# Windowed attention in three 128-row query-key passes, a quadrant output projection, single-window value steps and a new step order

## The chip, the cores and the metric

The kernel runs on one core of a Trainium2 chip. The metric is the device time of one execution in microseconds, the median of the runs shown. Engines are named as in the profile: PE (TensorE matmul), PEld (TensorE weight load), DVE (VectorE), ACT (ScalarE), POOL (GpSimd), SP (SyncE).

## The reference

Four residual layers act on x of shape (8, 56, 56, 192), each on a group-normalized copy of it. The change is in layer 1, a windowed attention with 7 x 7 windows, 6 heads of 32 channels and a shift of 3 rows and 3 columns. Its core, cut to what matters:

```python
x = (x - mu) * rsqrt(var + EPS) * gamma + beta            # over 192 channels
sx = roll(x, shift=(-3, -3))                               # rows, columns
win = windows of sx                                        # (windows, 49 tokens, 192)
q, k, v = split(win @ w_qkv + b_qkv)                       # 6 heads x 32 channels each
attn = (q * 32 ** -0.5) @ k.T + rel_bias + mask            # (49, 49) for each head and window
out = softmax(attn) @ v
out = out @ w_proj + b_proj                                # 192 to 192
x = x + roll(out, shift=(3, 3))
```

Everything is float32.

## The kernel before

The four layers run one after another as stages. Layer 1 takes about the stretch from 1985 to 3035 us of the profiled execution. An image lies in SBUF as 128 partitions: 64 channels of the upper image half (s = 0) on partitions 0 to 63 and the same channels of the lower half (s = 1) on 64 to 127, with three channel blocks j. A **group** g, one of four per image, is a strip of seven rows in each half: eight windows for each s. A window row of 49 tokens has two windows, z = 0 and 1, side by side in each of four slots k. So 8 images make 32 groups.

The steps of layer 1 have letters, and a string `plan` (line 1504) gives the order in which they are written down for one group:

- Q (`project(which, m)` in `layer1_scores`): queries or keys, 96 output rows at a time, so four steps per group. Each is 3 x 2 matmuls of 392 columns into two PSUM tiles of the tag `mm`, one for each s, and a copy of each into `qk`. Lines 877 (matmul), 883, 885 and 887 (copies).
- V (`values(k0)`): values of two slots, tokens on partitions. Lines 895 (matmul), 902 and 904 (copies).
- E (`scores(s)`): loads a bias-and-mask tile `bm` with a DMA on SP (line 910), 48 small matmuls into the single PSUM tile `S` (913), then on DVE the add of `bm` (919) and the row maximum (921), and on POOL the subtraction of the maximum (922).
- X (`exponents`): the exponential on ACT (926). Y (`shares`): sum and reciprocal on DVE (931, 932), scaling by the reciprocal on POOL (933).
- T (`turn`): transposes of the shares into PSUM tiles of the tag `et` (954), three steps for each s, the middle one evicted by DVE (961), the others by ACT (959).
- P (`mix`): shares times values into two `et` tiles (968), evicted into `oa` by ACT (979) and DVE (981).
- R (`project(j)` in `layer1_mix`): the output projection of one channel block (987), whose result DVE adds to `x` (995).
- G (`statistics`): group statistics of the strip on DVE (998).
- N: one step of `layer1_norm`, which prepares the next image: 33 steps per image. For strips 0 and 1 and then again for strips 2 and 3: four steps of window copies on POOL (eight instructions, 797), two steps of squares on ACT (804), both twice, and one step with the statistics matmuls (835, 839) and their reduction (850). Then three steps with clamp, square root and reciprocal (810, 812, 814), and four that multiply the image by it (819, 824). The normalization of image b+1 is spread over the groups 0, 1 and 2 of image b; image 0's lies ahead of the loop, and the last image's groups have none.

X, Y, T, P, R and G of a pass through the plan belong to group g, while Q, V and E already prepare group g+1. PE, ACT, DVE and POOL take their instructions strictly in the order in which the steps are written (`manual_schedule`), each engine from its own queue; DMAs have queues of their own. The tag `mm` has three PSUM tiles that rotate among Q, V, R, the statistics and the normalization's broadcasts (`rstd`); the tag `et` has two, which rotate among T and P. A tile is taken again only when the copies out of the tile three (or two) places earlier are done.

`layer1_weights` prepares weights and biases in layer 0's stage, and the host function at the end lays out the weights.

Of the kernel before, what the change touches and what calls it, by code (L numbers as in the profile page):

```python
# [19 lines left out]
HC = 96  # L20
# [9 lines left out]
HEADS, HD, WN = 6, 32, 49  # L30
PW, GW = 64 + WN, 4 * (64 + WN)
# [41 lines left out]
    ("g1", 3), ("be1", 3), ("bq", 2), ("bv", 2), ("bpr", 3),  # L73
# [18 lines left out]
def kernel(ctx: ExitStack, tc: tile.TileContext, a: dict, out: bass.AP):  # L92
# [603 lines left out]
    def layer1_weights(pool, psum):  # L696
# [9 lines left out]
        bv = pool.tile([HC, 2], F32, name="bv", bufs=1)  # L706
        for which, t in ((0, bq), (2, bv)):
            ps = psum.tile([128, 2, 512], F32, name="bias", tag="qv")[:, 0]
            for m in range(2):
                c0 = which * C + HC * m  # L710
                for j in range(3):
                    nc.tensor.matmul(
                        ps[0:HC, m:m + 1], w_qkv[0:64, j, c0:c0 + HC], vec("be1", j, 64), start=(j == 0), stop=(j == 2)
                    )
            o = VOFF["bq" if which == 0 else "bv"]
            nc.vector.tensor_tensor(t, ps[0:HC, 0:2], vecs[0:HC, o:o + 2], ALU.add)
# [3 lines left out]
        for s in range(2):  # L720
            for j in range(3):
                for m in range(2):
                    nc.tensor.matmul(
                        ps[64 * s:64 * s + 64, j:j + 1], w_proj[:, m, 64 * j:64 * j + 64], bv[:, m:m + 1],
                        start=(m == 0), stop=(m == 1),
                    )
# [4 lines left out]
        nc.vector.tensor_scalar(w_qkv[:, :, 0:C], w_qkv[:, :, 0:C], HD ** -0.5, None, ALU.mult)  # L731
# [132 lines left out]
    def layer1_scores(g, xr, pool, psum, S, es, consts):  # L864
# [3 lines left out]
        qk = [pool.tile([HC, 2, 2, TT], F32, name=f"qk{s}", bufs=1) for s in range(2)]  # L868
# [3 lines left out]
        def project(which, m):  # L872
            ps = [psum.tile([128, 512], F32, name="qk_ps", tag="mm", bufs=3)[0:HC, 0:TT] for s in range(2)]
            c0 = which * C + m * HC
            for j in range(3):
                for s in range(2):
                    nc.tensor.matmul(  # L877
                        in_pairs(ps[s]), wg[64 * s:64 * s + 64, j, c0:c0 + HC],
                        in_slots(xr[64 * s:64 * s + 64], (3 * g + j) * GW), start=(j == 0), stop=(j == 2),
                    )  # L880
            for s in range(2):
                if which == 0:
                    nc.scalar.activation(qk[s][:, 0, m], ps[s], AF.Identity, bias=bq[:, m:m + 1])
                elif s == 0:
                    nc.scalar.copy(qk[s][:, 1, m], ps[s])
                else:
                    nc.vector.tensor_copy(qk[s][:, 1, m], ps[s])

        def values(k0):
            ps = [psum.tile([128, 512], F32, name="v_ps", tag="mm", bufs=3)[:, 0:2 * C] for s in range(2)]  # L890
            for k in range(2):
                for j in range(3):
                    for s in range(2):
                        t0 = (3 * g + j) * GW + PW * (k0 + k)
                        nc.tensor.matmul(
                            ps[s][:, C * k:C * k + C], xr[64 * s:64 * s + 64, t0:t0 + 128],
                            wg[64 * s:64 * s + 64, j, 2 * C:3 * C], start=(j == 0), stop=(j == 2),
                        )
            for s in range(2):
                dst = v[s][:, k0:k0 + 2].rearrange("p w c -> p (w c)")  # L900
                if s == 0:
                    nc.scalar.copy(dst, ps[s])
                else:
                    nc.vector.tensor_copy(dst, ps[s])

        mxs = [None, None]
# [21 lines left out]
        def shares(s):  # L928
# [8 lines left out]
            Q=[lambda which=which, m=m: project(which, m) for which in range(2) for m in range(2)],  # L937
            V=[lambda k0=k0: values(k0) for k0 in (0, 2)], E=each(scores),
# [829 lines left out]
```

## Time and profile before

| | us |
|---|---|
| median of 3 runs | 5648.63 (5647.63 to 5649.4) |
| profiled execution, its own time | 5648.44 |
| its span, first to last instruction | 5646.6 |
| layer 1, about | 1985 to 3035 |
| PE busy in the span | 5131.2 (91%) |
| DVE busy | 3030.6 (54%) |
| ACT busy | 2287.3 (41%) |
| POOL busy | 1839.5 (33%) |
| mean granted TensorE clock | 0.961 |

The span is that of the profiled execution, from which all durations come. A matmul in float32 shows as two instructions, so 768 matmuls of a kind are 1536 rows. Busy PE counts overlapping matmuls once, and their ends are modelled, so the price of a step is better read from the start of one step to the start of the next. A row of a timeline gives start, duration, engine, line, operation, out<-in with shapes, the count, and in brackets the idle time of that engine just before and what ended it; neighbouring instructions of one line are merged into one row.

### The profile page before, as it was taken

Reading aid. Unit: us, or ns where it says so; the run is one execution under the profiler, and the core shown is the slowest. Engines: PE = TensorE matmul, PEld = TensorE weight load, DVE = VectorE, ACT = ScalarE, POOL = GpSimd, SP = SyncE. Lnnn points to the kernel's source line nnn. Section 1 sums busy time; section 2 is a strip of 40 time slices with the busy share of each in tenths; the row PEclk is TensorE's granted clock in tenths of the full one; section 3 lists DMA queues with packets and bytes.
Section 4 is the critical chain, followed back from the end, with each engine's and each line's share of the span. In section 5 each row is a group of like instructions: output and inputs, shape, how many; then the busy total and the mean of one; then the engine's idle time right before and its main releaser. Section 6 shows DMA issues by size and latency. Waiting matters only on the chain. (4 is left out here: it accounts for less than half of the span.)

```text
span 5646.6 us, 113339 instructions
## 1 busy us (share of the span) xinstructions
PE 5131.2 (91%) x49446; PEld 3421.6 (61%) x49446; DVE 3030.6 (54%) x4087; ACT 2287.3 (41%) x3100; POOL 1839.5 (33%) x1583
## 2 busy tenths in 40 slices
PE   7899969999999789999997989998888797999999
PEld 6798866666666445555554756775344697444444
DVE  4565534555554456556665868888787103433331
ACT  3344445555555333333331025554667201333333
POOL 5565655555555233334431023333010101101000
PEclk9999979999999889999998999999999898999999
DMA  5988996777777512223225756676677686212211
GB/s 148 235 226 227 223 299 245 272 273 272 273 273 274 151 36 80 74 73 81 75 62 144 266 213 228 231 241 190 185 205 212 247 330 257 78 59 78 80 39 26
DMA packets 556148, 1013.75 MB, mean 180 GB/s; under 512 B 256104, under 2 KB 479684, under 8 KB 528884
## 3 DMA queue, kind: packets, MB, share of 16 engines
q1 hardware_dynamic: 542896, 956.63, 52.8%
q0 software_dynamic: 8512, 40.62, 2.2%
q10 hardware_dynamic: 4244, 9.26, 0.6%
q8 instruction: 389, 6.37, 0.5%
q14 instruction: 107, 0.88, 0.0%
HBM read 676.92 MB, written 345.97 MB: 181 GB/s over the span
## 5 line engine op out<-in xcount | busy, mean ns | idle before, releaser
L460 POOL COPY lc<-lt 128x896 f32<-128x896 f32 (+1 forms) x320 | 590.3, 1854 | 542.8 <-PE op L468 506.6
L427 PE MATMUL qv<-w_qv_sb,x 64*112 64x256 f32 (+1 forms) x5376 | 685.7, 408 | 16.3 <-DVE act L433 12.4
L427 PEld LDWEIGHTS qv<-w_qv_sb,x 64*112 64x112 f32 x5376 | 600.2, 175 | 90.8 <-DVE act L433 22.6
L433 DVE TENSOR_TENSOR act<-qv,b_qv 112x640 f32<-112x640 f32 x448 | 318.8, 753 | 320.4 <-PE qv L427 245.0
L437 ACT ACTIVATE act<-act 112x640 f32<-112x640 f32 x448 | 300.6, 683 | 413.2 <-DVE act L433 402.7
L403 POOL TENSOR_TENSOR qv<-act 112x320 f32<-112x320 f32 x448 | 346.7, 798 | 288.4 <-ACT act L437 209.4
L468 PE MATMUL op<-rc,lc 128*56 128x56 f32 x9216 | 350.0, 221 | 61.5 <-POOL lc L460 33.0
L468 PEld LDWEIGHTS op<-rc,lc 128*56 128x56 f32 x9216 | 326.3, 135 | 129.5 <-POOL lc L460 56.6
L1361 PE MATMUL ph<-y,w_sb 64*128 64x392 f32 x2304 | 398.2, 498 | 6.5 <-ACT hid L1365 6.5
L1372 PE MATMUL po<-hid,w_sb 128*64 128x392 f32 x2304 | 386.3, 494 | 0.0
L1379 DVE TENSOR_TENSOR x<-x,z 128x392 f32<-128x392 f32 x96 | 69.6, 725 | 523.5 <-ACT z L1377 523.5
L1088 PE MATMUL cv<-zc,wt 128*128 128x224 f32 x1536 | 312.6, 355 | 25.3 <-DMA zc<-pd 24.6
L1088 PEld LDWEIGHTS cv<-zc,wt 128*128 128x128 f32 x1536 | 290.1, 189 | 68.8 <-issue 53.2
L877 PE MATMUL qk_ps<-xr,wg 64*96 64x392 f32 x1536 | 329.8, 531 | 1.7 <-DVE xr L824 1.7
L1361 PEld LDWEIGHTS ph<-y,w_sb 64*128 64x128 f32 x2304 | 220.2, 188 | 176.4 <-issue 26.1
L922 POOL TENSOR_TENSOR e<-e,mx 128x1176 f32<-128x1176 f32 x64 | 140.0, 2188 | 561.6 <-DVE mx L921 534.9
L478 PE MATMUL pj<-xn,w_p_sb 64*128 64x392 f32 x1536 | 288.8, 508 | 32.7 <-ACT pp L485 31.6
L1262 PE MATMUL cps<-zc,wt 128*128 128x224 f32 x1536 | 299.6, 356 | 18.0 <-DMA zc<-zd 15.9
L1103 POOL TENSOR_TENSOR rows<-rows,loc 128x896 f32<-128x896 f32 x96 | 218.8, 2279 | 274.7 <-ACT rows L1099 209.8
L1262 PEld LDWEIGHTS cps<-zc,wt 128*128 128x128 f32 x1536 | 289.6, 189 | 28.1 <-issue 20.5
L501 PE MATMUL y<-pp,w_o_sb 128*64 128x392 f32 x1536 | 301.2, 497 | 0.5 <-DVE pp L495 0.5
L460 DVE COPY rc<-rt 128x896 f32<-128x896 f32 (+1 forms) x160 | 215.3, 1346 | 150.4 <-PE op L468 96.8
(245 smaller groups left out, 8927.3 us busy)
## 6 DMA issues: line engine op xcount, KB each, us to landing
lt<-left SPq DMA_DIRECT2D x72, 1792.0 KB
rt<-right SPq DMA_DIRECT2D x72, 1792.0 KB
left<-qv SPq DMA_DIRECT2D x224, 252.0 KB
right<-qv SPq DMA_DIRECT2D x96, 504.0 KB
wt<-in_band_dram SPq DMA_DIRECT2D x23, 2048.0 KB
wt<-in_band_dram SPq DMA_DIRECT2D x11, 4096.0 KB
zc<-pd SPq DMA_DIRECT2D x187, 232.0 KB
pd<-pt SPq DMA_DIRECT2D x7, 5568.0 KB
```

The lines of the kernel that those rows point to most:

```text
L403: nc.gpsimd.tensor_tensor(qv[:, s, s0:s1, k], *(acts[s][:, which, 0:n].rearrange("p (s d) -> p s d", d=64) for which in range(2)), ALU.mult,)
L427: nc.tensor.matmul(ps[s][:, which, 0:n], x[64 * s:64 * s + 64, j, bass.ts(i, 2 * W)], w_qv[64 * s:64 * s + 64, j, which, 64 * s0:64 * s1], ...
L433: nc.vector.tensor_tensor(acts[s][:, :, 0:n], ps[s][:, :, 0:n], b_qv[:, :, 64 * s0:64 * s1], ALU.add)
L437: nc.scalar.activation(acts[s][:, :, 0:n], acts[s][:, :, 0:n], AF.Silu)
L460: copy(c[:, 0:nu], raw.rearrange("p (w u d) -> p u d w", u=nu, d=64 // nu)[:, :, d0:d0 + 8])
L468: nc.tensor.matmul(op[64 * u:64 * u + W, i, :], lc[:, u, i], rc[:, u, i], start=True, stop=True)
L501: nc.tensor.matmul(y[64 * s:64 * s + 64], w_o[:, 2 * g + u, 64 * j:64 * j + 64], pp[:, u, s], start=(u == 0), stop=(u == 1),)
L877: nc.tensor.matmul(in_pairs(ps[s]), wg[64 * s:64 * s + 64, j, c0:c0 + HC], in_slots(xr[64 * s:64 * s + 64], (3 * g + j) * GW), start=(j == ...
L1088: nc.tensor.matmul(dst, wt[:, c4 + i, 128 * q:128 * q + 128], zc[:, :, c4 + i, q:q + NPAIR], start=(q == 0), stop=(q == 1),)
L1262: nc.tensor.matmul(dst.rearrange("p (b n) -> p b n", n=NPAIR), wt[:, c4 + i, q * OP:(q + 1) * OP], zc[:, :, c4 + i, q:q + NPAIR], start=(q ...
L1361: nc.tensor.matmul(ps[:, s, 0:TT], w0[64 * s:64 * s + 64, j, m * 128:(m + 1) * 128], y[64 * s:64 * s + 64, j, ts], start=(j == 0), stop=(j ...
L1372: nc.tensor.matmul(ps[64 * s:64 * s + 64], w1[:, m, 64 * j:64 * j + 64], hid[:, m, s], start=(m == 0), stop=(m == 5),)
```

## The change

The columns of `w_qkv` are reordered on the host, so that queries and keys of a strip come out of **three passes of 128 rows** (Q three times per group). The constant MOVES says for each pass which rows are queries and which keys, and where they go in `qk`: in each pass ACT copies the queries, with their bias, and DVE the keys, from different rows of the same PSUM tile. `qk` keeps its layout, so E is as it was.

V works on **one slot at a time**, four steps per group, with copies of 192 columns.

P writes heads 0 to 3 of a slot on all 128 rows, and heads 4 and 5 on rows 0 to 63 (z = 0) or 64 to 127 (z = 1). So `oa` holds **128 channels for each z, and 64 channels of both z stacked on the partitions**. Each `po` tile is copied by one engine in two pieces.

R multiplies the 128 channels for each z with 196 columns (four matmuls), then the 64 remaining channels in **quadrants of 64 rows by 64 columns**, z choosing the rows and s the columns (four matmuls). The results of the two z lie in two PSUM tiles, one of the tag `mm` and one of the tag `et`, and DVE adds them to `x` in three pieces instead of two.

The plan has a new order, with three Q, four V and 13 instead of 14 N. Biases and weights are prepared for the new layouts.

```diff
+MOVES = (((0, 96, 0, 0), (96, 128, 64, 1)), ((96, 128, 64, 1), (0, 96, 0, 0)), ((0, 64, 0, 1), (64, 128, 0, 1)))
...

         wg, bq = consts[0:2]
-        qk = [pool.tile([HC, 2, 2, TT], F32, name=f"qk{s}", bufs=1) for s in range(2)]
+        qk = [pool.tile([96, 2, 2, TT], F32, name=f"qk{s}", bufs=1) for s in range(2)]

         v = [pool.tile([128, 4, C], F32, name=f"v{s}") for s in range(2)]

-        def project(which, m):
-            ps = [psum.tile([128, 512], F32, name="qk_ps", tag="mm", bufs=3)[0:HC, 0:TT] for s in range(2)]
-            c0 = which * C + m * HC
+        def project(m):
+            ps = [psum.tile([128, 512], F32, name="qk_ps", tag="mm", bufs=3)[:, 0:TT] for s in range(2)]
             for j in range(3):
                 for s in range(2):
                     nc.tensor.matmul(
-                        in_pairs(ps[s]), wg[64 * s:64 * s + 64, j, c0:c0 + HC],
+                        in_pairs(ps[s]), wg[64 * s:64 * s + 64, j, 128 * m:128 * m + 128],
                         in_slots(xr[64 * s:64 * s + 64], (3 * g + j) * GW), start=(j == 0), stop=(j == 2),
                     )
             for s in range(2):
-                if which == 0:
-                    nc.scalar.activation(qk[s][:, 0, m], ps[s], AF.Identity, bias=bq[:, m:m + 1])
-                elif s == 0:
-                    nc.scalar.copy(qk[s][:, 1, m], ps[s])
-                else:
-                    nc.vector.tensor_copy(qk[s][:, 1, m], ps[s])
-
-        def values(k0):
-            ps = [psum.tile([128, 512], F32, name="v_ps", tag="mm", bufs=3)[:, 0:2 * C] for s in range(2)]
-            for k in range(2):
-                for j in range(3):
-                    for s in range(2):
-                        t0 = (3 * g + j) * GW + PW * (k0 + k)
-                        nc.tensor.matmul(
-                            ps[s][:, C * k:C * k + C], xr[64 * s:64 * s + 64, t0:t0 + 128],
-                            wg[64 * s:64 * s + 64, j, 2 * C:3 * C], start=(j == 0), stop=(j == 2),
-                        )
-            for s in range(2):
-                dst = v[s][:, k0:k0 + 2].rearrange("p w c -> p (w c)")
-                if s == 0:
-                    nc.scalar.copy(dst, ps[s])
-                else:
-                    nc.vector.tensor_copy(dst, ps[s])
-
-        mxs = [None, None]
+                for i, (p0, p1, to, slot) in enumerate(MOVES[m]):
+                    dst, src = qk[s][to:to + p1 - p0, i, slot], ps[s][p0:p1]
+                    if i == 0:
+                        nc.scalar.activation(dst, src, AF.Identity, bias=bq[p0:p1, m:m + 1])
+                    else:
+                        nc.vector.tensor_copy(dst, src)
+
+        def values(k):
+            ps = [psum.tile([128, 512], F32, name="v_ps", tag="mm", bufs=3)[:, 0:C] for s in range(2)]
+            for j in range(3):
+                for s in range(2):
+                    t0 = (3 * g + j) * GW + PW * k
+                    nc.tensor.matmul(
+                        ps[s], xr[64 * s:64 * s + 64, t0:t0 + 128], wg[64 * s:64 * s + 64, j, 2 * C:3 * C],
+                        start=(j == 0), stop=(j == 2),
+                    )
+            nc.scalar.copy(v[0][:, k], ps[0])
+            nc.vector.tensor_copy(v[1][:, k], ps[1])

         def scores(s):
             bm = pool.tile([128, 24, WN], F32, name="bm")
...

         each = lambda f: [lambda s=s: f(s) for s in range(2)]
         return v, dict(
-            Q=[lambda which=which, m=m: project(which, m) for which in range(2) for m in range(2)],
-            V=[lambda k0=k0: values(k0) for k0 in (0, 2)], E=each(scores),
+            Q=[lambda m=m: project(m) for m in range(3)], V=[lambda k=k: values(k) for k in range(4)], E=each(scores),
         ), dict(X=each(exponents), Y=each(shares))

     def layer1_mix(g, x, v, pool, psum, es, consts, st):
...

         w_proj, bpr = consts[2:4]
         ets = [pool.tile([128, 12, 128], F32, name="et") for _ in range(2)]
-        oa = [pool.tile([HC, 2, TT], F32, name=f"oa{s}", bufs=1) for s in range(2)]
+        oa = [pool.tile([128, 3, 4 * WN], F32, name=f"oa{s}", bufs=1) for s in range(2)]

         def turn(s, i):

...

         def mix(s):
             et = ets[s]
-            po = [psum.tile([128, 512], F32, name="po", tag="et", bufs=2)[0:HC, 0:TT] for _ in range(2)]
-            for y, p, hh, r, z in np.ndindex(2, 2, 2, 3, 2):
+            po = [psum.tile([128, 512], F32, name="po", tag="et", bufs=2) for _ in range(2)]
+            for y, p, h, z in np.ndindex(2, 2, HEADS, 2):
                 k = 2 * y + p
+                row, col = (HD * h, 0) if h < 4 else (64 * z + HD * (h - 4), 4 * WN)
                 nc.tensor.matmul(
-                    po[z][32 * r:32 * r + 32, 4 * WN * hh + WN * k:4 * WN * hh + WN * k + WN],
-                    v[s][64 * z:64 * z + WN, k, HC * hh + HD * r:HC * hh + HD * r + HD],
-                    et[64 * z:64 * z + WN, 4 * r + 2 * hh + y, 64 * p:64 * p + WN],
+                    po[z][row:row + HD, col + WN * k:col + WN * k + WN],
+                    v[s][64 * z:64 * z + WN, k, HD * h:HD * h + HD],
+                    et[64 * z:64 * z + WN, 4 * (h % 3) + 2 * (h // 3) + y, 64 * p:64 * p + WN],
                     start=True, stop=True,
                 )

             for z in range(2):
-                dst = oa[s][:, :, 4 * WN * z:4 * WN * (z + 1)]
-                src = po[z].rearrange("p (m n) -> p m n", m=2)
-                if z == 0:
-                    nc.scalar.copy(dst, src)
-                else:
-                    nc.vector.tensor_copy(dst, src)
+                copy, rows = (nc.scalar.copy, nc.vector.tensor_copy)[z], slice(64 * z, 64 * z + 64)
+                copy(oa[s][:, z], po[z][:, 0:4 * WN])
+                copy(oa[s][rows, 2], po[z][rows, 4 * WN:8 * WN])
+
+        by_row = lambda z: z.rearrange("p (w i j) -> p i w j", i=7, j=7)

         def project(j):
-            ps = psum.tile([128, 512], F32, name="pr", tag="mm", bufs=3)[:, 0:TT]
-            for m in range(2):
+            out = []
+            for z, (tag, bufs) in enumerate((("mm", 3), ("et", 2))):
+                out.append(psum.tile([128, 512], F32, name=f"pr{z}", tag=tag, bufs=bufs)[:, 0:4 * WN])
                 for s in range(2):
                     nc.tensor.matmul(
-                        ps[64 * s:64 * s + 64].rearrange("p (i w j) -> p i w j", i=7, j=7),
-                        w_proj[:, m, 64 * j:64 * j + 64],
-                        oa[s][:, m].rearrange("p (w i j) -> p i w j", i=7, j=7), start=(m == 0), stop=(m == 1),
-                    )
-            rows = ps.rearrange("p (i w) -> p i w", w=W)
-            for w0, w1, c0 in ((0, 53, 3), (53, 56, 0)):
+                        out[z][64 * s:64 * s + 64].rearrange("p (i w j) -> p i w j", i=7, j=7),
+                        w_proj[:, 0, 64 * j:64 * j + 64], by_row(oa[s][:, z]), start=True, stop=False,
+                    )
+            for z in range(2):
+                rows = slice(64 * z, 64 * z + 64)
+                for s in range(2):
+                    nc.tensor.matmul(
+                        out[z][64 * s:64 * s + 64].rearrange("p (i w j) -> p i w j", i=7, j=7),
+                        w_proj[rows, 1, 64 * j:64 * j + 64], by_row(oa[s][rows, 2]), start=False, stop=True,
+                    )
+            for z, w0, w1, c0 in ((0, 0, 28, 3), (1, 0, 25, 31), (1, 25, 28, 0)):
                 xs = x[:, j, 7 * g:7 * g + 7, c0:c0 + w1 - w0]
-                nc.vector.scalar_tensor_tensor(xs, rows[:, :, w0:w1], bpr[:, j:j + 1], xs, ALU.add, ALU.add)
+                src = out[z].rearrange("p (i w) -> p i w", w=28)[:, :, w0:w1]
+                nc.vector.scalar_tensor_tensor(xs, src, bpr[:, j:j + 1], xs, ALU.add, ALU.add)

         def statistics(j):
             nc.vector.bn_stats(st[:, j, g], x[:, j, 7 * g:7 * g + 7].rearrange("p h w -> p (h w)"))
...
-        for kind in "QVQVQQEE":
+        for kind in "QVVQVVQEE":
             ahead[kind].pop(0)()
             for _ in range(4):
                 next(own, None)
         run(own)

 
-        plan = "X Q Y V X G Q Y N T T T N Q N P N G V N N T T T N G N N P N Q N R N E N R G E N R".split()
+        plan = "X Q Y V X G V Q Y N T T T N V N P N G N N T T T N Q N P N G V N E N R N R G E N R".split()
...
+    heads = np.r_[0:96, 352:384, 192:288, 160:192, 96:160, 288:352, 384:576]
...
-    halves = lambda w: w.reshape(2, HC, -1).transpose(1, 0, 2)
+    w_proj = l1("w_proj")
+    w_proj = np.stack([w_proj[0:128], np.tile(w_proj[128:C], (2, 1))], axis=1)
```

In the preparation of `layer1_weights` the scaling of the query columns becomes two instructions instead of one, and the additions of the biases five instead of two.

## The prediction

> **What bounds the kernel now.** I read the page's busy times, then stretches inside layer 1 (1985 to 3035 us), then each engine's timeline of two groups.
>
> ```profile
> PE 5131.2 (91%) x49446; PEld 3421.6 (61%) x49446; DVE 3030.6 (54%) x4087; ACT 2287.3 (41%) x3100; POOL 1839.5 (33%) x1583
> ```
> ```profile
> 2384.01:2412.07 28.06, 26.60 (x531) 16.26 (x529) 16.94 (x26) 9.77 (x16) 8.77 (x5) 1.00 0.23 68
> 2412.07:2446.50 34.43, 30.63 (x556) 17.64 (x554) 19.36 (x28) 13.80 (x23) 17.74 (x23) 0.96 0.55 127
> 2349.30:2384.01 34.71, 31.58 (x538) 17.83 (x536) 25.40 (x35) 10.42 (x17) 8.77 (x5) 0.95 0.19 56
> ```
> The second view has one group per row: length, busy PE, PEld, DVE, ACT, POOL, granted clock. A group without norm steps (N) lasts 28.06 us, with TensorE busy 26.60: TensorE sets the pace. Groups with N add 6 to 7 us. Each image but the last has groups g0 and g1 with window copies, squares and statistics, g2 with the reciprocal, and g3 without N.
>
> TensorE's timeline of the 28.06 us group gives the price of a step, from its start to the next one's:
>
> ```profile
> 2393.56 2.22 PE L877 MATMUL qk_ps<-xr,wg 64*96 64x392 f32 x12
> 2395.71 1.09 PE L968 MATMUL po<-et,v 49*32 49x49 f32 x96
> 2396.73 2.22 PE L895 MATMUL v_ps<-wg,xr 64*128 64x192 f32 x24
> 2398.88 1.09 PE L954 MATMUL et_ps<-ident,e 128*128 128x128 f32 x8
> ...
> 2402.55 2.22 PE L877 MATMUL qk_ps<-xr,wg 64*96 64x392 f32 x12
> 2404.70 1.66 PE L987 MATMUL pr<-oa,w_proj_sb 96*64 96x392 f32 x8
> 2406.29 1.36 PE L913 MATMUL S<-qk 32*49 32x49 f32 x96
> 2407.59 1.66 PE L987 MATMUL pr<-oa,w_proj_sb 96*64 96x392 f32 x8
> ```
> So Q 2.15, P 1.02, V 2.15, R 1.59, E 1.30; three T take 1.92. The pairs of Q's weight loads come every 0.33 us: a pair of 392 columns streams in 0.327, and a step costs 0.2 (R 0.28) above its streams.
>
> The softmax chain runs beside this. Where it has slack shows in g0 (POOL, ACT, then PE):
>
> ```profile
> 2420.50 2.19 POOL L933 TENSOR_TENSOR e<-e,sm 128x1176 f32<-128x1176 f32 x1 [1.32 <-ACT qk L883]
> 2422.67 8.31 POOL L797 TENSOR_SCALAR xr<-x,scsh 128x196 f32<-128x196 f32 x16
> ```
> ```profile
> 2427.41 1.30 ACT L804 ACTIVATE sq<-xr 128x588 f32<-128x588 f32 x2
> 2428.61 0.58 ACT L959 COPY et<-et_ps 128x512 f32<-128x512 f32 x1
> ```
> ```profile
> 2419.69 1.09 PE L954 MATMUL et_ps<-ident,e 128*128 128x128 f32 x8
> 2426.94 1.09 PE L954 MATMUL et_ps<-ident,e 128*128 128x128 f32 x8
> 2428.82 0.66 PE L954 MATMUL et_ps<-ident,e 128*128 128x128 f32 x4 [0.78 <-DVE et L961]
> ```
> POOL scales the second half's shares (end 2422.69), then copies windows; eight copies (half of 8.31, 4.15) end at 2426.8. ACT squares them and only then evicts the second TTT, which began at 2426.94. Third transpose: 0.55 late. This fits with under a microsecond to spare.
>
> [...] in g2 a low stretch of transposes and a wait of 1.19 us ends in a Q of 3.91 us instead of 2.22.
>
> ```profile
> 2358.55 0.66 PE L954 MATMUL et_ps<-ident,e 128*128 128x128 f32 x4 [0.24 <-ACT et L959]
> 2360.39 0.92 PE L819 MATMUL rstd<-rs,sel 32*128 32x392 f32 x2 [1.19 <-DVE rs L814]
> 2361.24 3.91 PE L877 MATMUL qk_ps<-xr,wg 64*96 64x392 f32 x12
> ```
> [...]
>
> **The change, part by part.**
> Queries and keys: one Q of four goes, -2.15 us. The weight load is 128 columns instead of 96; V's 128-column load takes 187 ns, under the 0.327 stream: nothing (bound +0.03 a pair if that cover is gone). Evictions per group go from ACT 6, DVE 2 to 6 and 6: DVE +4 x 0.48 (its interval in a queue) = +1.9 us.
> Values: 24 matmuls (12 pairs x 0.163) become two steps of six pairs, 0.98 + 0.2 each: between +0[...] and +0.2 per former V. [...]
> Output: eight instructions of 392 become eight of 196 (4 x 0.163) and eight in quadrants (2 x 0.163 if four run at once)[...]: 0.65 + 0.2 + 0.33 + 0.28 = 1.46 against 1.59, -0.13. Unseen: [...]1.8 if quadrants go in pairs. DVE takes three pieces (196, 175, 21) for two: by 598 ns at 371 and 229 at 21, 0.76 against 0.65. [...]
> Order: V is split around P and ends before E; two R stand between the E's. E's mask load on SP is issued about 25 us before its use: nothing; if that cover went, up to 7.3 us, what a copy of its size takes to land in the DMA issues. Bias and weight preparation in stage 0, a dozen small instructions, under 1 us beside busy TensorE. Prologue and tail: -2 together.
>
> TensorE's content thus falls by about 2.4 us a group. **What is late next** I set down with t=0 at the start of a group's first E, all engines in written order, intervals as DVE's and POOL's rows of before have them: an E's add starts 1.41 after it, the maximum 1.48 later, the next copy 1.30 later; POOL subtracts 1.52 after the maximum's start (2.19), ACT's exponential follows (1.21).
> DVE: add 1.41, max 2.89, R 4.19, R 4.95, second add 5.71, max 7.19, R 8.49, two copies of Q from 9.29, sum 10.25, reciprocal 11.65 to 11.95, V to 12.33. POOL: subtractions end at 6.60 and 10.90; exponentials end at 7.84 and 12.45.
> TensorE: E 0, R 1.30, R 2.76, E 4.22, R 5.52, Q 6.98 to 9.13. A step of Q or V takes two of three `mm` buffers, so its second half waits for an eviction of the step before: V for Q's, on both engines, until 9.95; the next V for the first one's on ACT, 11.4; Q for V's, behind the second exponential on ACT, 12.8. T comes at 15.0. In before it comes 13.4 after its E, with one R less: stalls of 1.7 for 1.2.
> Now the second sum stands on DVE behind two copies of that second Q. In before only ACT evicted it, and the sum began 1.06 us ahead of T (2390.58 against 2391.64); now at 15.76, behind it. The reciprocal ends at 17.46, POOL's scaling runs 17.56 to 19.75, and DVE's TTT eviction waits until 18.17. TensorE: T to 17.1, V, P 18.25, second TTT 20.05 to 21.85, Q, P, V, and the next E at 26.1. **A clean group: 26.1 for 28.06, -1.95.**
>
> In g0 and g1 the windows follow the scaling: 19.75 + 4.15 = 23.9, squares 1.3, eviction 0.6: third transpose at 25.8 instead of 21.3, +4.5 (before: 0.55 and about 0.4). TensorE idles 4.7 us, so the half clock follows; before shows it in spells near 3.4 and 6.8 us, costing half of the work in them. I take 1.7, bounds 0 and 3.4. So g0: -1.95 + 4.0 + 1.7 = +3.75; g1 +3.85. In g2 reciprocal and rstd move behind V and P: the reciprocal ends at 22.15, TensorE waits 2.6, DVE's four products hold the third Q; group 34.3 for 34.7, -0.4 (bounds -2 and +3).
>
> Sum: ten clean groups (seven g3, three of the last image) -19.5; seven images x (3.75 + 3.85 - 0.4) = +50.4; ends -2: **+29**. I take +24, as the half clock will miss some. The profiled execution took 5648.44 us (span 5646.6 and 1.8 around it), the median is 5648.63: no correction. Forecast 5672.
>
> **The rivals.** (1) Faster: the second scaling isn't late, windows stay hidden. For: TensorE is the pace-maker and loses 2.4 us a group. Against: the written order puts Q's copies ahead of the second sum. 31 groups x -1.95, less 1.55 x 7 in g2, ends -2: -52, 5597. It decides if the third transpose of g0 is late by under 2 us. (2) The stall comes, the half clock costs nothing: +29 - 24 = +5, 5654, no measurable change. (3) Worse: quadrants run in pairs (+0.34 x 96 = +33) or spells of 6.8 us in g0 and g1 (+1.7 x 14 = +24): about 5700.
>
> **Chances.** The forecast with (3) 0.62, (2) 0.12, (1) and mixtures with part of the stall 0.26. A measurement tells about 0.2%, 11 us, from no change. Slower 0.62, same 0.12, faster 0.26. The range 5594 to 5702 holds (1) at its centre and leaves out what lies beyond it, and the worse part of (3); the forecast's own is 5660 to 5702.
>
> **What would show it.** Right: clean groups near 26.1; in g0 and g1 the third transpose of the second TTT waiting 3 to 5 us for ACT, squares waiting for POOL, a slow Q behind; R near 1.46; DVE copies of Q just ahead of the sum. Wrong: POOL's second scaling starting before T, g0 shorter than 34.4, the clock in layer 1 as before, or ACT and DVE taking turns on one bank.

## The result, and the profile after

The changed kernel took 5727.92 us (5725.96 to 5735.61, four runs) beside 5649.01 us for the kernel before on the same chip: ratio 1.0142, 95% interval 1.0124 to 1.0159. It is slower by 79 us, where the forecast was 23 us and its range ended at 5702. The profiled execution after is 5735.61 us long (span 5733.8).

From the page of the kernel after, the busy times:

```profile
PE 5113.6 (89%) x49836; PEld 3473.5 (61%) x49836; DVE 3122.7 (54%) x4443; ACT 2294.9 (40%) x3228; POOL 1837.1 (32%) x1583
```

TensorE is busy 18 us less, and yet the span is 87 us longer: its idle time grew by 105 us. The stretches of one group each, from the first transpose of one group to that of the next (length, busy PE, PEld, DVE, ACT, POOL, granted clock), here g1, g2, g3 and the next image's g0:

```profile
2366.57:2403.93 37.36, 29.65 (x567) 19.32 (x565) 20.38 (x37) 13.00 (x26) 16.20 (x20) 0.91 0.20 56
2403.93:2439.35 35.42, 31.26 (x550) 20.19 (x548) 28.12 (x46) 13.06 (x23) 8.74 (x4) 0.86 0.18 53
2439.35:2466.78 27.43, 24.90 (x542) 17.02 (x540) 19.73 (x36) 10.07 (x20) 9.44 (x6) 1.00 0.23 69
2466.78:2506.97 40.19, 31.08 (x567) 19.73 (x565) 20.86 (x38) 12.99 (x26) 16.19 (x20) 0.87 0.43 107
```

Only the clean group is shorter than before. Means over the seven images that have all four kinds (the last image has no N), in us, before and after: g0 35.0 and 37.6, g1 30.8 and 36.9, g2 33.7 and 35.8, g3 28.05 and 27.7. From the first transpose of layer 1 to the end of its last it is 992.3 us before and 1062.9 after. The mean granted clock over layer 1's groups is 0.97 before and 0.92 after.

The stall that was forecast is there. POOL, ACT and PE of the g1 that follows these rows, as timelines:

```profile
2510.43 2.19 POOL L926 TENSOR_TENSOR e<-e,sm 128x1176 f32<-128x1176 f32 x1 [3.80 <-DVE sm L925]
2512.60 8.27 POOL L798 TENSOR_SCALAR xr<-x,scsh 128x196 f32<-128x196 f32 x16
```
```profile
2516.78 1.30 ACT L805 ACTIVATE sq<-xr 128x588 f32<-128x588 f32 x2 [4.22 <-POOL xr L798]
2517.98 0.56 ACT L951 COPY et<-et_ps 128x512 f32<-128x512 f32 x1
```
```profile
2512.67 1.09 PE L946 MATMUL et_ps<-ident,e 128*128 128x128 f32 x8 [0.67 <-POOL e L926]
2518.60 1.12 PE L946 MATMUL et_ps<-ident,e 128*128 128x128 f32 x4 [4.83 <-ACT et L951]
2519.64 4.29 PE L877 MATMUL qk_ps<-xr,wg 64*128 64x392 f32 x12
```

The second half's scaling on POOL begins with the transposes that wait for it, the first eight window copies follow it, ACT's squares wait 4.22 us for those, and the eviction that the third transpose needs stands behind the squares. TensorE idles 4.83 us, and the Q behind that takes 4.29 us instead of 2.25. All seven g0 and all seven g1 have this wait, of 4.82 or 4.83 us; in g0 the Q takes 3.2 to 3.9. At each of these stalls the granted clock is 0.50 for 6.83 us, beginning before the wait ends, here (the same columns):

```profile
2517.01:2523.84 6.83, 5.24 (x16) 2.59 (x16) 0.00 (x0) 2.12 (x4) 3.46 (x8) 0.50 0.01 2
```

I estimate the cost of such a stretch at half clock, a spell, as half of TensorE's work in it, here 2.6 us of 5.24; the rest of the 6.83 us falls into the wait.

The output projection came out better than forecast. R in the timeline, ahead of the clean group's first transpose (2439.35):

```profile
2425.52 0.94 PE L980 MATMUL pr<-oa,w_proj_sb 128*64 128x196 f32 x8
2426.39 0.59 PE L987 MATMUL pr<-oa,w_proj_sb 64*64 64x196 f32 x8
2426.91 0.94 PE L980 MATMUL pr<-oa,w_proj_sb 128*64 128x196 f32 x8
```

From start to start 0.87 for the 128 channels and 0.52 for the quadrants: 1.39 where 1.46 was forecast (0.85 and 0.61, an estimate: the steps of before, with four quadrants at once) and 1.59 was before. Eight instructions in quadrants take less than the eight ahead of them.

Outside the groups the kernel lost too. In layer 0's stage, the preparation of biases:

```profile
254.19 1.41 PE L712 MATMUL bias<-vecs_sb,w_qkv_sb 64*128 64x1 f32 x6 [18.16 <-issue]
255.85 1.43 PE L712 MATMUL bias<-vecs_sb,w_qkv_sb 64*128 64x1 f32 x6 [0.25 <-DVE bq L715]
257.54 2.72 PE L712 MATMUL bias<-vecs_sb,w_qkv_sb 64*128 64x1 f32 x12 [0.25 <-DVE bq L715]
```

Each block of bias columns has an add of its own on DVE, and the next block writes the same PSUM tile, so it waits for that add. From the first bias matmul to the last it is 19.8 us before and 22.8 after; in the later variants with the same preparation (e1, e2, e3, e5 and e8 to e12 below) it is 22.9 to 24.2, and in e7, whose preparation is that of before, 18.6. So about 3 to 5 us belong to the change. The last of the `qv` matmuls behind it ends at 763.0 us before and 774.2 after, and in e7 at 765.5: the rest of these 11 us is not explained. The prologue of layer 1, from the last add of layer 0 on DVE to the first transpose, takes 79.4 us instead of 75.0.

### The profile page after: what moved, and what is told of

Read it like the earlier page. It is cut to its first block, busy times and chain, and to the rows that moved or that the text cites. A ratio compares the mean times of both kernels' runs of the same rounds, so it can differ in the third digit from the quotient of the medians.

```text
span 5733.8 us, 114622 instructions
## 1 busy us (share of the span) xinstructions
PE 5113.6 (89%) x49836; PEld 3473.5 (61%) x49836; DVE 3122.7 (54%) x4443; ACT 2294.9 (40%) x3228; POOL 1837.1 (32%) x1583
## 5 line engine op out<-in xcount | busy, mean ns | idle before, releaser
L468 PE MATMUL op<-rc,lc 128*56 128x56 f32 x9216 | 349.0, 221 | 65.0 <-POOL lc L460 35.1
L478 PE MATMUL pj<-xn,w_p_sb 64*128 64x392 f32 x1536 | 289.5, 509 | 29.8 <-ACT pp L485 28.5
L1371 PEld LDWEIGHTS po<-hid,w_sb 128*64 128x64 f32 x2304 | 162.6, 137 | 213.8 <-issue 213.8
```

What stands on the lines that cost most here:

```text
L468: nc.tensor.matmul(op[64 * u:64 * u + W, i, :], lc[:, u, i], rc[:, u, i], start=True, stop=True)
L478: nc.tensor.matmul(ps[:, s, 0:TT], w_p[64 * s:64 * s + 64, j, 128 * c:128 * c + 128], xn[64 * s:64 * s + 64, j, bass.ts(t, TT)], start=(j ...
L1371: nc.tensor.matmul(ps[64 * s:64 * s + 64], w1[:, m, 64 * j:64 * j + 64], hid[:, m, s], start=(m == 0), stop=(m == 5),)
```

## Experiments

Each kernel was timed beside the kernel before, whose medians in these series lie between 5647 and 5650 us, so a difference of a few us between two variants says little. Group lengths are means over seven images from one profiled execution; that of e2 was 16 us longer than e2's median, that of e8 13 us longer, that of after 8.

| kernel | median us | ratio to before, 95% interval | g0 | g1 | g2 | g3 |
|---|---|---|---|---|---|---|
| before | 5649.0 | 1 | 35.0 | 30.8 | 33.7 | 28.05 |
| after | 5727.9 | 1.0142 [1.0124, 1.0159] | 37.6 | 36.9 | 35.8 | 27.7 |
| e1 one reader | 5721.0 | 1.0129 [1.0113, 1.0144] | 37.4 | 36.4 | 35.1 | 27.3 |
| e2 sum first | 5665.9 | 1.0042 [1.0028, 1.0057] | 34.9 | 32.6 | 36.1 | 27.3 |
| e3 squares later | 5661.2 | 1.0020 [1.0011, 1.0028] | 31.6 | 30.6 | 37.8 | 27.7 |
| e4 output alone | 5636.4 | 0.9977 [0.9971, 0.9984] | 33.4 | 30.4 | 33.5 | 27.8 |
| e5 both orders | 5637.2 | 0.9983 [0.9976, 0.9990] | 30.6 | 29.3 | 37.9 | 27.4 |
| e6 passes alone | 5663.4 | 1.0033 [1.0020, 1.0046] | 31.8 | 38.9 | 29.7 | 28.0 |
| e7 values alone | 5673.8 | 1.0049 [1.0034, 1.0064] | 35.1 | 31.6 | 34.1 | 28.9 |
| e8 passes, output | 5651.8 | 1.0009 [1.0002, 1.0016] | 31.8 | 39.1 | 28.9 | 27.2 |
| e9 spaced | 5628.4 | 0.9963 [0.9950, 0.9975] | 30.5 | 29.3 | 36.5 | 27.1 |
| e10 late reciprocal | 5662.3 | 1.0026 [1.0015, 1.0036] | 30.9 | 29.3 | 41.0 | 27.4 |
| e11 spaced, V in two | 5623.4 | 0.9956 [0.9941, 0.9971] | 32.4 | 33.7 | 30.6 | 27.2 |
| e12 first pair | 5605.7 | 0.9923 [0.9897, 0.9949] | 29.8 | 28.8 | 36.0 | 26.7 |

**e1: one engine for each of Q's PSUM tiles.** In after, ACT and DVE read different rows of one tile. ACT and DVE at the second Q of the clean group:

```profile
2439.40 1.05 ACT L885 ACTIVATE qk<-qk_ps,bq 32x392 f32<-32x392 f32 x2 [2.27 <-PE qk_ps L877]
```
```profile
2440.01 1.03 DVE L887 COPY qk<-qk_ps 96x392 f32<-96x392 f32 x2 [2.21 <-ACT qk L885]
2440.97 1.36 DVE L924 TENSOR_REDUCE sm<-e 128x24 f32<-128x1176 f32 x1
```

DVE starts 0.61 us after ACT, when ACT has done with the first tile (0.58 us a copy). In this program the two engines take turns, by a wait that ends with ACT's copy; whether the chip would allow both at once was not tried.

```diff
-                    if i == 0:
+                    if s == 0 and i == 0:
                         nc.scalar.activation(dst, src, AF.Identity, bias=bq[p0:p1, m:m + 1])
+                    elif s == 0:
+                        nc.scalar.copy(dst, src)
+                    elif i == 0:
+                        nc.vector.tensor_scalar(dst, src, bq[p0:p1, m:m + 1], None, ALU.add)
                     else:
                         nc.vector.tensor_copy(dst, src)
```

> The changed kernel, except that each PSUM tile of a Q step has one reader: ACT takes both pieces of the tile s = 0, DVE both pieces of s = 1 (its queries with the bias added). The number of copies per engine stays. Theory 'turns': two engines reading one PSUM tile take turns (in the changed kernel DVE's copy starts 0.61 us after ACT's), which costs a clean group 1.3 us (second scaling 1.0 earlier, last V 0.4): 31 groups x 1.3 = 40 us less than the changed kernel's 5728, about 5690, the DVE copies starting with ACT's. Rival 'load': DVE is late because it has 40% more copies, whoever reads what: within 8 us of 5728.

Measured: 7 us less than after, where the two intervals overlap; clean groups 0.4 shorter, g0 and g1 within 0.5 of after. The turns delay the second sum by little: DVE's two pieces, now free to start, take 1.23 us in a row. As the main cause this theory falls. The rival's number held; its reason, the number of copies, was not tested.

**e2: the second sum ahead of the second Q.**

```diff
-plan = "X Q Y V X G V Q Y N T T T ...
+plan = "X Q Y V X G V Y Q N T T T ...
```

> The changed kernel with one swap in the plan: the second Y (row sums on DVE, scaling on POOL) ahead of the second Q instead of after it. Theory 'late scaling': the sum moves from 16.7 to about 13.2 us after the group's first E, so POOL's second scaling, the windows and the squares come 3.5 earlier; the third transpose of the second TTT waits about 1.3 instead of 4.8 us in g0 and g1, the slow Q (4.29 instead of 2.25) goes with it, clean groups lose their 0.66 waits: 14 x (3.5 + 2) + 31 x 1 = some 100 us less than 5728, about 5630. Rival: the stall is DVE's or POOL's load as such, the order does not matter: 5715 to 5730.

**e3: the second half's transposes ahead of two N.**

```diff
-... N P N G N N T T T N Q N ...
+... N P N G T T T N N N Q N ...
```

> The changed kernel with the two N steps that hold the squares in g0 and g1 moved from ahead of the second TTT to behind it; the second scaling stays late. Theory 'squares block the eviction': the third transpose waits 0.3 us instead of 4.8, the next Q runs at 2.25 instead of 4.29; the squares now delay the copies of that Q by about 1 us: 14 x (4.5 + 2.0 - 0.8) = 80 us less than 5728, about 5648. Rival 'windows hold POOL': the wait for POOL moves to another ACT instruction and costs the same: 5715 to 5730. If the half clock comes of itself with this much idle TensorE, the stall goes and the slow Q stays: about 5676.

**e5: both.**

> The kernel after with both reorderings at once: in the order list the first 'Q Y' pair of a group is exchanged (a Y, the sum with its scaling, goes ahead of the second Q) and the three transposes of the second half go ahead of two of the N (norm) slots. Theory 'order': the loss sits in the two stalls, each reordering removes its own, so they add up in part: sum first gave -62, squares later -67, and since both also repair the same g1 stall the two together give about -95 against after, 5633 us. Rival 'content': g2's new stall behind rstd, which the later squares brought (37 to 38 us against 35.6), stays whatever the sum does, and g1 cannot go below its 30.7: then 5655 to 5661. Below 5640 speaks for the first, above 5650 for the second.

Measured: 62, 67 and 91 us less than after, where 100, 80 and 95 were expected. Each edit alone takes most of the stall out of g1 (36.9 to 32.6 and 30.6); together 29.3, a group with N that is less than 2 us above a clean one. So the stall is the chain of the second sum, the scaling, the windows and the squares, and breaking it at either end works.

e2 leaves a wait of about 2.0 us at the third transpose, and in 11 of the 14 g0 and g1 the Q behind it is still slow, which fits its falling short. One of them on PE:

```profile
2320.59 1.12 PE L946 MATMUL et_ps<-ident,e 128*128 128x128 f32 x4 [2.02 <-ACT et L951]
2321.64 4.29 PE L877 MATMUL qk_ps<-xr,wg 64*128 64x392 f32 x12
```

In e3 and e5 that wait is 0.24 us and the Q behind it takes 2.25 in all 14. Their g0 also falls 3 to 4 us below the kernel before (31.6 and 30.6 for 35.0): before has spells of its own in six of seven g0, mostly at the second E, and in e3 and e5 nearly all of these are gone too. That part of the gain is not the stall's, and why it came was not tested. e3 and e5 make g2 longer by 2 us: there the three N ahead of Q are three of the four multiplications by the normalization's factor, and Q waits for DVE to free their PSUM tiles, 1.74 or 1.75 us in each g2 of e5. To that extent e5's rival was right.

**e4: the output part alone, put into before.** The edit is that of P, R and their layouts in the change's diff, of which R's core is:

```diff
-                        w_proj[:, m, 64 * j:64 * j + 64],
+                        w_proj[:, 0, 64 * j:64 * j + 64], by_row(oa[s][:, z]), start=True, stop=False,
...
+                        w_proj[rows, 1, 64 * j:64 * j + 64], by_row(oa[s][rows, 2]), start=False, stop=True,
```

> The kernel before with the output part alone: heads 0 to 3 on 128 rows and heads 4 and 5 stacked, P with two copies per tile, R as four matmuls of 128 channels and four in quadrants, DVE adding three pieces; Q, V and the plan as before. Theory 'R pays': R 1.39 instead of 1.59 us, 96 of them: -19 us, with +2 for the weight preparation and some 5 for the added copies: 5636, that is 0.998 of the kernel before. Rival 'DVE gives it back': three pieces and four more copies per group delay the adds of E and the TTT evictions: no gain or up to 15 us slower.

Measured: 13 us less, as 'R pays' had it: 0.3 to 0.4 in a clean group and in g1. R's three shares of 0.20 would be 0.6; where the rest of it goes was not tested. The largest part in the profile is 1.7 in g0, whose length varies with the spells, so that the sum came out right is in part luck.

**e7: values in four steps, put into before.** V's edit is that of the change's diff, with two V in the plan where there was one:

```diff
-            V=[lambda k0=k0: values(k0) for k0 in (0, 2)], E=each(scores),
+            V=[lambda k=k: values(k) for k in range(4)], E=each(scores),
...
-plan = "X Q Y V X G Q Y N T T T N Q N P N G V N N ...
+plan = "X Q Y V V X G Q Y N T T T N Q N P N G V V N N ...
```

> From before: only the values, in four single slots in place of two double ones, in the same places of the order (two V next to each other wherever one stood). The prediction put this edit at nothing. Theory 'nothing': 5649 within 0.2%. Rival 'more waits': twice as many V steps, each with its own tile and eviction, leave TensorE 0.2 to 0.6 us per group more: 5655 to 5670.

Measured: 26 us more, 0.9 in the clean group, more than the rival had. The two V, one behind the other, on PE, with ACT's first copy of them:

```profile
2282.51 2.89 PE L894 MATMUL v_ps<-wg,xr 64*128 64x192 f32 x24
```
```profile
2283.78 0.32 ACT L898 COPY v<-v_ps 128x192 f32<-128x192 f32 x1 [0.70 <-PE v_ps L894]
```

In before 24 such matmuls took 2.22 in one step. Stretches of 0.2 us show where the difference lies (V's matmuls alone: busy time, and in brackets how many are active):

```profile
2283.60:2283.80 0.20, 0.20 (x4) 1.00 0.00 0
2283.80:2284.00 0.20, 0.20 (x2) 1.00 0.00 0
2284.00:2284.20 0.20, 0.12 (x3) 1.00 0.00 0
2284.20:2284.40 0.20, 0.20 (x2) 1.00 0.00 0
2284.40:2284.60 0.20, 0.20 (x6) 1.00 0.00 0
```

From 2283.8 to 2284.4 only two or three are active, where the stream that follows has six. A step takes two of the three `mm` tiles, so the second V's second tile is the first V's first, and ACT copies that until 2284.10. The row of 24 hides this in its busy time. This pair accounts for 0.66 of the 0.9 us (2.81 from its start to the next step's, for 2.15).

**e6 and e8: three passes, without and with the new output; V in two steps.** Into before go Q's edit from the change's diff, and in e8 also e4's; both have 15 N per group.

```diff
-plan = "X Q Y V X G Q Y N T T T N Q N P N G V N N T T T N G N N P N Q N R N E N R G E N R".split()
+plan = "X Q Y V X G Y Q N T T T N V N P N G T T T N N N Q N P N G N N N R N E N R G E N R".split()
```
 (In e6's expectation, the 32 groups are those of all eight images.)

> From before: only the three passes for queries and keys (128 rows each), with values in their two steps and the output projection of 96 plus 96 rows as before; order with the sum ahead of the second Q and the transposes ahead of two N. Theory 'the passes pay': one Q of 2.15 us less per group and one eviction group fewer on ACT and DVE, 2 us less in a clean group; with 32 groups in a layer-1 image pair and no stall this is 5649 minus 30 to 60, 5590 to 5620. Rival 'the copies give it back': each of the three Q is evicted as two pieces that take 1.2 us on DVE one after the other, the later evictions hold V and the second sum, and the group stays at 28: 5640 to 5665.

> e6 plus the new output projection (128 rows plus 64 in quadrants), values left in two steps. Theory 'parts add up': the output part alone gave -13 (ratio 0.9977), so e6 minus 13; with e6 at about 5605 this is about 5592, faster than both kernels. Rival 'they collide': the third P eviction or R's second tile takes from the same PSUM buffers as the transposes and costs what the shorter R gave: equal to e6 within 5 us, or slower.

Measured: 16 us more than before for e6, 12 us less than e6 for e8. The output part adds up as in e4. e6 came out where its rival had it, with a clean group of 28.0 us, but the trace shows another loss than the copies: my plan put R right behind P. Its clean group on PE:

```profile
2290.36 1.09 PE L966 MATMUL po<-et,v 49*32 49x49 f32 x96
2291.39 0.93 PE L985 MATMUL pr<-oa,w_proj_sb 96*64 96x392 f32 x2
2292.86 1.64 PE L985 MATMUL pr<-oa,w_proj_sb 96*64 96x392 f32 x6 [0.55 <-DVE oa L979]
```

R waits for P's evictions and takes 3.04 us (2291.39 to 2294.43) instead of 1.59. And g1 stalls, 38 to 39 us: with 15 N the norm's end falls there. No kernel has the passes with R elsewhere and all else as before, so what the passes are worth alone stays open.

**e9, e10, e11: the norm's tail.** In e5 the reciprocal is written one N ahead of its first user, the `rstd` matmul, and PE waits for it in every g2 (20.4 us in seven waits). e9 (on e5) and e11 (on e8) leave one N idle behind it and give each product two N; e10 puts square root and reciprocal later.

```diff
         yield from finish(slice(0, 128))
+        yield
         for g in range(4):
+            yield
             scaled(g)
             yield
```

> Both reorderings (the kernel with the sum first and the squares later, 5637 us) with the end of the norm spread out: after the reciprocal one N slot does nothing, and each of the four scalings of the next image's windows (rstd matmul, two multiplications on DVE) gets two N slots in place of one. Theory 'the norm's tail': group g2 takes 37 to 39 us where a group without N takes 27, of which about 3 us is TensorE waiting for the reciprocal, 2.3 us Q waiting for the multiplications to free its PSUM buffers, and 2 us the half clock behind those waits; apart, most goes, 5 to 7 us over 7 images: 5637 minus 35 to 50, 5587 to 5602 us. Rival: the same waits return one by one, since DVE does the same 2.6 + 6 us of work between copies that TensorE waits for: 5625 to 5640.

> The same base, the norm's tail put later instead of spread: square root at the fifth N slot, behind the second half's transposes, reciprocal at the eighth, the four scalings one per slot at the ninth to twelfth. Theory 'the norm's tail': the copies of P ahead of the second transposes no longer queue behind a reciprocal of 2.6 us on DVE, and the rstd matmul has a V step of cover: 5590 to 5605 us. Rival: the scalings now fall among V, E and R, which take PSUM buffers from the same three, so that each waits for DVE: 5625 or more.

> Three passes and the new output projection, values in two steps (5652 us), with the same spreading of the norm's tail as in e9. Here the groups after the norm's tail already take 28.8 us and the stall sits in g1 (38 to 40 us). Theory 'the norm's tail': rstd wait (2.7 us) and the half clock behind it go, g1 to 32 to 34 us: 5652 minus 30 to 40, 5612 to 5622 us. Rival: the cost is only moved to g2, 5645 to 5655.

Measured: 9 us less than e5, 25 us more than e5, 28 us less than e8. The theory held in the main for e11, where g1 goes from 39.1 to 33.7 while g2 gains 1.7; it falls for e10, and e9 gives a quarter of what was expected. In e10 the reciprocal stands behind DVE's copies of the last Q, which come late, and is done only when `rstd` has waited 3.35 us. DVE and PE there:

```profile
2374.92 1.05 DVE L892 COPY qk<-qk_ps 64x392 f32<-64x392 f32 x2 [3.14 <-ACT qk L890]
2375.89 2.59 DVE L815 RECIPROCAL rs<-rs 128x392 f32<-128x392 f32 x1
```
```profile
2378.54 0.92 PE L820 MATMUL rstd<-rs,sel 32*128 32x392 f32 x2 [3.35 <-DVE rs L815]
2386.48 1.58 PE L985 MATMUL pr<-oa,w_proj_sb 128*64 128x196 f32 x8
```

The first part of R takes 1.58 instead of 0.94: up to 2396 the whole stretch of E, R and V is slow, which with the wait makes g2 41 us long. In e9 no `rstd` waits for the reciprocal, but g2 keeps 36.5. Its longest wait ahead of the slow stretch is 0.95 us, of the first transpose for P's copies on ACT; the reciprocal (2.60 us) stands on DVE ahead of P's other copies, which end at 2359.82 and let the third transpose start at 2359.88. From the second transpose on TensorE is slow, and the Q behind still takes 3.63 us. What would mend that was not tried.

**e12: the first two V of e9 in one step again, the other two alone.**

```diff
-V=[lambda k=k: values(k) for k in range(4)]
+V=[lambda k=k: values(*k) for k in ((0, 1), (2,), (3,))]
...
-plan = "X Q Y V X G V Y Q N ...
+plan = "X Q Y X G V Y Q N ...
```

> The kernel with both reorderings and the norm's tail spread out (5628 us), with the first two of its four values steps made one step again (two slots into one pair of PSUM tiles, two copies of 384 columns in place of four of 192), at the second one's place, behind the exponential and the statistics; the third and the fourth step stay alone. Theory 'buffers turn': a values step takes two of the three PSUM buffers that it shares with Q and R, so of two steps next to each other the second waits for the first one's copy; 24 matmuls take 2.8 to 3.2 us so and 2.2 to 2.5 in one step. One such pair per group gone: 0.5 to 0.7 us in each of 32 groups, 5628 minus 16 to 22, 5606 to 5612 us. Rival 'it only moves': behind the pair come Q and the transposes that wait for the second sum and its scaling, so that TensorE is early and waits there: 5623 to 5633 us, as values in two steps came out equal to values in four in the new order (27.2 against 27.0 us in a clean group).

Measured: 5605.73 us (5598.9 to 5619.03), 23 us less than e9 and 0.8% less than before, at the lower edge of what 'buffers turn' forecast (5606). Each kind of group is 0.4 to 0.75 us shorter, 16 us over layer 1 in the two profiles; the rest of the 23 is not explained. g0 and g1 of one image, at the full clock, and its g2 (the same columns as above):

```profile
2289.26:2317.79 28.53, 26.46 (x566) 17.63 (x565) 20.81 (x38) 13.13 (x26) 16.22 (x20) 1.00 0.56 142
2317.79:2346.77 28.98, 26.79 (x566) 17.98 (x565) 20.43 (x37) 13.14 (x26) 16.19 (x20) 1.00 0.26 73
2346.77:2382.44 35.67, 31.16 (x549) 19.93 (x548) 29.51 (x46) 13.05 (x23) 8.75 (x4) 0.90 0.18 53
```

The third row, g2, is what is left: DVE has 29.5 us of work there, and the granted clock is 0.90. PE in it:

```profile
2351.97 0.63 PE L951 MATMUL et_ps<-ident,e 128*128 128x128 f32 x4 [0.69 <-ACT oa L976]
2353.28 0.66 PE L951 MATMUL et_ps<-ident,e 128*128 128x128 f32 x4 [0.68 <-ACT et L956]
2354.52 0.66 PE L951 MATMUL et_ps<-ident,e 128*128 128x128 f32 x4 [0.59 <-DVE oa L976]
2355.11 0.92 PE L820 MATMUL rstd<-rs,sel 32*128 32x392 f32 x2
2355.96 3.94 PE L879 MATMUL qk_ps<-xr,wg 64*128 64x392 f32 x12
```

No wait there is longer than 0.69 us, and Q is slow all the same.

## Why the prediction was wrong

**The mechanism of the stall was right.** Squares behind windows behind a late scaling: forecast 4.7 us of idling, measured 4.83; e2 and e3 show that it is the order, as both relieve it. The half clock behind it: 1.7 forecast, about 2.5 measured in g1 (Q 4.29 for 2.25, the transposes ahead of it 1.12 for 0.66). For a half clock behind an idle TensorE the prediction shows one case, the wait of 1.19 us in g2 of before; its price was an estimate. R: 1.46 forecast, 1.39 measured.

**The first step that failed is "A clean group: 26.1 for 28.06, -1.95".** It measured 27.7 on average, -0.3. In the group whose rows are shown above the next E comes 27.44 us after the first (2424.22 to 2451.66), 1.34 behind the forecast:

```profile
2445.05 1.09 PE L946 MATMUL et_ps<-ident,e 128*128 128x128 f32 x8 [0.66 <-POOL e L926]
2450.21 1.51 PE L894 MATMUL v_ps<-wg,xr 64*128 64x192 f32 x12
2451.66 1.37 PE L906 MATMUL S<-qk 32*49 32x49 f32 x96
```

- Up to the first transpose the sum held: T at 15.13, forecast 15.0. It held with estimated lengths for the shorter copies: V's of 192 columns take 0.36 us on DVE and 0.32 on ACT (medians), and P's of 196 as much.
- The second sum starts at 16.75 instead of 15.76. I let DVE's copies of Q start with ACT's, which no row of before shows for one tile, and follow at 0.48; they start 0.61 later, and in e1, without that wait, they still take 1.23 for two. Second transposes at 20.83 instead of 20.05. Either remedy, e1 or e2, is worth 0.4 in a clean group.
- Behind these transposes 0.56 more is lost, mostly by V: 1.44 from its start to E's, where half of 2.15 was forecast.

**Values "between +0 and +0.2 per former V" was mis-sized**, the lower end being an estimate: alone they cost 0.9 per group (e7), most of it by the turn of the three tiles. I had that wait in the sum for the first pair of V, as one of the stalls before T, and did not see that the split made it: e12 undoes it and gains 0.4 in a clean group.

**The second step that failed is the half clock, put at 1.7 in g0 and in g1 and at nothing in g2.** Estimated as above from the two profiles, the spells cost, per group before and after, 2.3 and 2.4 us in g0, 0 and 2.65 in g1, 1.0 and 4.3 in g2. In g0 the change adds almost nothing: the spells that before has there of its own (without one, its g0 lasts 30.6 us, with one 34.4 to 37.4) are gone in four of six images, and the stall brings others. In g2 the wait was right in size (2.6 forecast, 2.27 measured here), but with it a spell of 10.2 us begins (2411.19 to 2421.43):

```profile
2411.50 1.68 PE L820 MATMUL rstd<-rs,sel 32*128 32x392 f32 x6 [2.27 <-DVE rs L815]
2413.11 2.91 PE L946 MATMUL et_ps<-ident,e 128*128 128x128 f32 x12
2415.95 1.67 PE L820 MATMUL rstd<-rs,sel 32*128 32x392 f32 x2
2417.55 4.50 PE L877 MATMUL qk_ps<-xr,wg 64*128 64x392 f32 x12
```

**Ends -2** was wrong in sign. The two profiles differ by 16 us outside the groups: 11 up to the end of the `qv` matmuls, of which 3 to 5 are the bias preparation, 4 in the rest of layer 0, whose code is unchanged, 4 in the prologue, and -3 behind layer 1. I had priced the preparation by its number of instructions, and it costs by the waits between them. The prologue's part was not tested by itself; in e7, with the values alone, it is 81.0 us long.

**The sum.** By groups, forecast and measured change in us: g0 +3.75 and +2.6; g1 +3.85 and +6.0; g2 -0.4 and +2.1; g3 -1.95 and -0.3. The profiled executions are 87 us apart, 58 more than the sum's 29: 36 from the seven images (7 x (-1.2 + 2.2 + 2.5 + 1.6)), 4 from the last image and 18 from outside the groups. By the estimate above 18 to 19 of the 40 inside the groups are the half clock; the rest is mostly what the clean groups and g1 show. So no single term carries the miss.

Two readings in the prediction were off without harm: of the groups with N, g1 lasted only 30.8 us before, 2.8 and not 6 to 7 above a clean one; and of the last image's three groups one is not clean, as its g0 also holds group statistics of the images before it (35.3 us before, 34.7 after).

**The rivals.** (1), windows stay hidden, 5597: not what happened, but e5 and e12 build it; the hidden stall alone gives 5637, and 5606 comes only with the first V pair merged and the norm spread. (2), no cost of the half clock, is refuted by the slow Q; by the estimate the spells of the seven images cost 42 us more than before. (3), quadrants in pairs or 6.8 us spells: R excludes the first. The second came true in length, in all g0 and g1, but not at its price of 3.4 us: 1.2 to 3.8 us of each spell fall into the wait, which leaves 1.5 to 2.8 us.

## What to carry to other kernels

The step that was split here cost by what it waits for, not by its matmuls (0.66 of 0.9 us a group at one pair of V): count the buffers that two neighbours need at once, and follow their turn, before splitting it to save elsewhere. Where engines take their work in written order, follow each long chain over all queues (here DVE's sum, POOL's scaling and windows, ACT's squares and eviction) to the first instruction that TensorE needs. The dramatic stall was forecast well; the miss came from smaller terms that every group or every image repeats: the step between two copies in a queue, the slow clock behind a short wait (2.27 us in g2), preparation priced by its number of instructions.

## What the runs showed of the hardware

A drop to half clock needs no long idling here: in g2 of before the granted clock is 0.50 from 2361.60 to 2364.50 us, in the Q behind a wait of 1.19 us. Q takes 4.29 us instead of 2.25 behind 4.83 us of idling and also behind 2.02 (e2), and 3.94 in e12 behind transposes with three waits of 0.6 to 0.7 us. In the seven images of after the spells last 3.4, 6.8 or 10.2 us. Nor do they end soon where short waits follow: in e10 R is still slow 8 us after its wait of 3.35 us. With the stalls gone, the g0 and g1 of e12 shown above run at a granted clock of 1.00.

Float32 matmuls of 64 rows by 64 columns, placed in the four quadrants, run beside each other: in R's rows shown above all eight instructions are active from 2426.65 to 2426.75 us, where of the first part's eight four are active from 2426.00 to 2426.10. The eight of 196 columns take 0.52 us from start to start, the eight that use all 128 rows 0.87.
